# Layer 0 of a four-layer graph network on one core: pair 3 normalised ahead of pair 2 and turned through DRAM, the adjacency's squares turned and written later

## The chip, the cores and the metric

The kernel runs on one core of a Trainium2 chip. The number that counts is device microseconds of one execution, as a median over several; four runs of the kernel before gave 964.04, 964.34, 964.43 and 965.01 us, median 964.38 us. The engines are named as in the profile: PE (matrix products and their weight loads, PEld), DVE (VectorE), ACT (ScalarE), POOL (GpSimd), SP (the engine that issues all the DMAs here).

## What is computed

`x` is 32 graphs of 512 nodes with 128 features, `adj` one 512x512 matrix that all graphs share. Four layers follow each other, each of the form `x = x + layer(relu(layernorm(x)), adj)`. Only layer 0 is touched:

```
h = jnp.maximum(_layernorm(x, axis=-1), 0.0)
# layer 0, with h as input
h0 = jnp.einsum('bnf,fg->bng', input, W[0])
h1 = jnp.einsum('bnf,fg->bng', input, W[1])
m = adj > 0
idx = jnp.cumsum(m.reshape(-1).astype(jnp.int32)) - 1
vals = e[0][idx].reshape(adj.shape)
A = jnp.where(m, vals, jnp.float32(NEG))
A = jax.nn.softmax(A, axis=1)
M = jnp.eye(adj.shape[0], dtype=A.dtype)
out = jnp.einsum('ij,bjg->big', A * M, h0) + jnp.einsum('ij,bjg->big', A * (1.0 - M), h1)
return out + bias[None, None, :]
```

Layer 1 is a Chebyshev filter on `adj`, layer 2 message passing with `adj` squared element by element, layer 3 attention whose weights are multiplied by `adj` (there the transposed `adj` is needed, which layer 0 prepares).

## The kernel before, in words

Two graphs make a pair, so there are 16 pairs, 0 to 15. A quad tile of `x` holds two pairs; layer 0 handles one such tile in each of eight rounds (`round0(r)`, pairs A = 2r and C = 2r + 1).

What one pair needs in layer 0, in this order:

- its statistics (`stats_steps`): four `bn_stats` on DVE (L227), a square root on ACT (L233), then a reciprocal (L235) and the shift `sh` (L236) on DVE;
- the normalised tile `h` (`normed_steps`, L247): eight activations on ACT, four for each graph;
- the same with features on the partitions, `hT`. This is made in one of two ways. `pe_steps` (L261) does eight 128x128 transposes on PE into two PSUM banks (L265) and two copies out of them (L268). `turn_steps` (L278) turns 32x32 squares on DVE, two instructions (L283), writes them with four DMAs into a bounce buffer in DRAM (L290) and reads the whole back with one DMA (L292);
- its projection `g = h W[1]` (`project_steps`): sixteen products on PE (L435) into two banks, two copies on ACT (L460);
- with the round's other pair, four block differences of `g` on POOL (`right_steps`, L356), and `hd`, `hT` scaled by the diagonal of A (`straight`, L703), also on POOL.

A round multiplies the off-diagonal attention by `g` with seven block products instead of eight (Winograd's form); the left sums are made once, the right differences per round. A product with number k goes into bank a, c or d (`ORDER`, L359), and `evict` (L782) takes it out on DVE. Bank c is used three times in a round: product 7 is added on top of product 6 only after DVE has read product 6 out (L787), and product 4 on top of product 7 only after L791. The order on PE in round 0 is 1, 2, 6, 5, 7, 4, 3, and 1, 6, 5, 7, 2, 4, 3 in the others. Between the products come the projections of the next round's pairs and the products with the diagonal (L759).

The order of the instructions in layer 0 is written out by hand: `manual_schedule` (L166) keeps PE, DVE, ACT and POOL in program order, and the loop over `products` in `round0` says at each index i what is issued after the product. The DMAs around the change are kept in program order on SP's queue too. Each engine runs its own list in order, so an instruction that waits holds up all that stands behind it on that engine.

In the kernel before, pairs 0 to 3 are turned on PE and pairs 4 to 15 through DRAM. Pair 2's statistics run ahead of pair 3's (`early_stats_2`, then `ln3`). `turn_adj` (L479) turns `adj` in 32x32 squares: four DVE instructions (L484) and four DMAs to DRAM (L488), all within the preparation and round 0. From round 3 on POOL changes `adj_s` in place for layer 1 (`late_sums`), and the tile `adj_squares` shares its memory with the last tile of `x`, which is loaded at the end of round 3.

Of the kernel before, what the change touches and what calls it, by code (L numbers as in the profile page):

```python
# [24 lines left out]
def kernel(  # L25
# [37 lines left out]
    nc = tc.nc  # L63
    B, N, D = x.shape
    NT = N // P
# [192 lines left out]
    def feature_major(name):  # L258
        return work.tile([P, NQR, 2, P], F32, tag="hT", name=name, bufs=4)
# [53 lines left out]
    def att_copies(*which):  # L313

        for j, half, copy in which:
            copy(attT[:, j, half * H : half * H + H], pt[j][:, half * H : half * H + H])
# [150 lines left out]
    def go(steps, n=99):  # L467
        for _ in range(n):
            if next(steps, steps) is steps:
                return  # L470
# [8 lines left out]
    def turn_adj():  # L479


        ab = last.tile([P, N // QR, NT, QR], F32, tag="x", name="adj_squares")
        for t in range(NT):
            nc.vector.transpose(ab[:, :, t, :], adj_s[:, t, :].rearrange("p (j c) -> p j c", c=QR))  # L484
            yield
        for b in range(NQR):
            tc.keep_in_program_order(
                nc.sync.dma_start(adjT_d[:, blk(b)].rearrange("(j r) e -> r j e", r=QR),  # L488
                                  ab[b * QR : (b + 1) * QR].rearrange("r j t c -> r j (t c)")))
        yield  # L490

# [62 lines left out]
            nc.gpsimd.tensor_sub(ecoln, ecoln, part)  # L556
        parts.append(part)
    h = {q: normed_tile(q) for q in range(3)}
    hT = {q: feature_major(f"hT0_{q}") for q in range(4)}
    normal = [normed_steps(q, h[q]) for q in range(3)]  # L560
    go(normal[0])

# [81 lines left out]
    def scaled_rows(t):  # L644
# [5 lines left out]

    attT = square_tile("attT")
    squares = turn_adj()
    early_stats_2 = stats_steps(2)
    score_rows(0)
    softmax_rows(0)
    next(project[0])
# [13 lines left out]
    softmax_rows(3)  # L670
    inverse(2)
    scaled_rows(2)
    go(early_stats_2, 2)
    inverse(3)
    scaled_rows(3)
    next(project[1])
# [5 lines left out]
    next(left_of_att)  # L682
    att_copies((0, 0, nc.scalar.copy), (1, 0, nc.vector.tensor_copy),
               (2, 0, nc.scalar.copy), (3, 0, nc.scalar.copy))
    go(early_stats_2, 3)
    next(squares)
    go(right_of(0))

    prep_scope.close()
# [30 lines left out]
        tc.keep_in_program_order(nc.gpsimd.tensor_scalar(th[:, 2, :], th[:, 2, :], 2.0, None, OP.mult))  # L720

    ahead = {q: stats_steps(q) for q in range(4, NQ)}
    ln3 = stats_steps(3)
    own, turning, hd, adiag = {}, {}, {}, []
    sums_ahead = late_sums()

    def normalise(q):
        h[q] = normed_tile(q)
        go(normed_steps(q, h[q]))
# [6 lines left out]
        return turning[q]  # L736

    def projection(q):
        return project_steps(q, hT[f"hT0_{q}"] if q > 3 else hT[q])

    def diagonal_of(r, b):
        for q in (2 * r, 2 * r + 1):
            src = hT[f"hT0_{q}"] if q > 3 else hT[q]
            hd[q, b] = straight(src, b, adiag[0], f"hd_{q}_{b}")

    def x_block(r, I, b):
# [15 lines left out]
    def round0(r):  # L762
# [41 lines left out]
        def upper(p):  # L804
            diagonal(p, 0, 0, False)
            nc.vector.tensor_add(x_of(0, 0), of_pairs(halves(p)), x_of(0, 0))

        def add(I, b, i):
            nc.gpsimd.tensor_add(x_of(I, b), x_of(I, b), of_pairs(u[i]))
# [5 lines left out]
        for i, _ in enumerate(products(f"l0_{r}", by_token, sums["att"], now, evict,  # L815
                                          ORDER if r else ORDER0)):
            if r == 0:
                if i == 0:
                    transpose_rows(pt, att, 2)
                    transpose_rows(pt, att, 3)  # L820
                    att_copies((0, 1, nc.scalar.copy), (1, 1, nc.vector.tensor_copy))
                    next(left_of_att)
                    next(left_of_att)
                    go(early_stats_2)
                    att_copies((2, 1, nc.scalar.copy), (3, 1, nc.scalar.copy))
                elif i == 1:
                    for t in range(NT):
                        nc.tensor.matmul(p_adiag[:, blk(t)], ones, diag[:, t, :], start=True, stop=True)
                    nc.scalar.copy(adiag[0], p_adiag)  # L829
                    go(normal[2], NT + 1)  # L830
                    diagonal_of(0, 0)
                    go(ln3, NT + 1)
                    go(normal[2])
                    next(left_of_att)
                    next(left_of_att)
                    next(squares)
                    go(ln3)
                elif i == 2:
                    diagonal_of(0, 1)
                    add(1, 0, 0)  # L840
                elif i == 3:
                    next(turned[2])
                    go(turned[2])
                    add(0, 1, 1)
                    bias(0)
                    normalise(3)
                    go(ahead[4], NT)
                    go(squares)
                elif i == 4:
                    upper(held["a"])  # L850
                    turned.append(pe_steps(h[3], "hT0_3", hT[3]))
                    next(turned[3])
                    go(ahead[4])
                    add(1, 1, 2)
                    go(turned[3])
                    go(projection(2))
                    normalise(4)
                    go(ahead[5], NT)
                    bias(1)
                    go(turn(4))  # L860
                    go(ahead[5])
                elif i == 5:
                    go(projection(3))
                    go(right_of(1))
                    diagonal_of(1, 0)
                    normalise(5)
                elif i == 6:
                    go(stats_c, NT)
                continue
            if i == 0:  # L870
                if C + 2 < NQ:
                    go(turn(C + 2))
                if A + 4 < NQ:
                    normalise(A + 4)
                diagonal_of(r, 1)
                add(1, 0, 0)
            elif i == 1:
                add(0, 1, 1)
                go(stats_a, NT + 1)
                go(own_a, NT)  # L880
                if more:
                    bias(r + 1)
                go(stats_a)
                go(own_a)
            elif i == 2:
                if more:
                    go(projection(A + 2))
            elif i == 3:
                add(1, 1, 2)
                if not more:  # L890
                    next(next_layer)
                if C + 4 < NQ:
                    normalise(C + 4)
                if r >= 3:
                    go(sums_ahead, 2)
            elif i == 4:
                if A + 4 < NQ:
                    go(turn(A + 4))
            elif i == 5:
                if more:  # L900
                    go(projection(C + 2))
                    go(right_of(r + 1))
                    diagonal_of(r + 1, 0)
                go(stats_c, NT + 1)
                go(own_c, NT)
            elif i == 6:
                go(stats_c)
        p = bank(f"p_l0_{r}_e")
        diagonal(p, 1, 1, True)
        nc.vector.tensor_add(x_of(1, 1), of_pairs(halves(p)), x_of(1, 1))  # L910
# [285 lines left out]
```

## Time and profile before

| | before |
|---|---|
| median of four runs | 964.38 us |
| profiled execution, its own time | 964.04 us |
| its span | 962.2 us |
| PE busy | 953.4 us (99%) |
| PEld (weight loads, beside PE) | 781.0 us (81%) |
| DVE / ACT / POOL busy | 585.3 / 469.6 / 421.6 us |
| granted TensorE clock, mean | 0.999 |
| one execution of layer 0: rounds 0 to 7 | from about 29 to 184 us of the span |

Times in the timeline are microseconds from the start of the span: start, duration, engine, line, operation, and what is written and read. Instructions that follow each other with the same line and shape are merged (x8), and an engine's next start can lie a little before the end of the last one, since they are pipelined. A square bracket at the end tells how long the engine sat idle before it and what ended that. SPq lines are the issuing of a DMA, not its data.

### The profile page before, as it was taken

How to read it: one execution, taken by the hardware profiler on the slowest of the kernel's cores; microseconds unless marked ns; L12 is line 12 of the kernel's file. 1: busy time of each engine (PE TensorE's matmuls, PEld its weight loads, DVE VectorE, ACT ScalarE, POOL GpSimd, SP SyncE). 2: the span in 40 equal slices, each digit the busy share in tenths (PEclk: the TensorE clock that was granted, in tenths of full speed). 3: DMA queues.
4: the chain of work that ended last, by engine and by line, in shares of the span. 5: the costliest groups of instructions: out<-in, count | busy, mean ns of one | idle time of the engine just before them, and what ended most of it. 6: DMA issues, size and time to landing. Idle time of an engine off the chain costs nothing.

```text
span 962.2 us, 15160 instructions
## 1 busy us (share of the span) xinstructions
PE 953.4 (99%) x5468; PEld 781.0 (81%) x5469; DVE 585.3 (61%) x1332; ACT 469.6 (49%) x1055; POOL 421.6 (44%) x463
## 2 busy tenths in 40 slices
PE   8999999999999999999999999999999999999998
PEld 4899999898989999899878777777677777767776
DVE  8878885846536546657667665665654444444444
ACT  5865442442232233277627655444765445544553
POOL 4878987833517522513333444433032223223322
PEclk9999999999999999999999999999999999999999
DMA  9257533341341230443333432223121121211111
GB/s 254 59 158 193 154 111 87 98 113 54 105 137 43 68 88 23 110 110 94 87 101 99 126 89 86 70 85 88 55 89 56 56 77 44 76 57 45 55 33 44
DMA packets 83913, 86.04 MB, mean 89 GB/s; under 512 B 6784, under 2 KB 74624, under 8 KB 83840
## 3 DMA queue, kind: packets, MB, share of 16 engines
q1 hardware_dynamic: 83840, 85.09, 31.6%
q8 instruction: 43, 0.70, 0.3%
q14 instruction: 30, 0.25, 0.1%
HBM read 44.17 MB, written 40.89 MB: 88 GB/s over the span
## 4 chain that ended last, share of the span: by engine, by line
PE 96%; ACT 1%; DMA 1%; DVE 1%; issue 0%; SPq 0%; DVEq 0%; ACTq 0%
PE p_av L1116 12%; PE p_score L1101 11%; PE p_l_c L386 8%; PE p_w L435 6%; PE p_l_d L386 6%; PE p_msgT_c L379 5%; PE p_l_a L386 4%; PE p_x1T_c L379 4%; PE p_l L435 3%; PE p_feat L435 3%; PE p_hv L435 3%; PE p_msgT_d L379 3%; PE p_msgT_a L379 3%; PE p_phi L1071 3%; PE p_qkh L1088 3%; PE p_phi L1072 3%
## 5 line engine op out<-in xcount | busy, mean ns | idle before, releaser
L247 ACT ACTIVATE h<-x,sh,rs 128x128 f32<-128x128 f32 x512 | 209.1, 485 | 50.9 <-PE p_x1T_d L379 21.6
L1106 POOL TENSOR_TENSOR ex<-ex,adjTx 128x512 f32<-128x512 f32 x62 | 80.4, 1297 | 208.2 <-ACT ex L1104 208.2
L1102 ACT ACTIVATE ex<-p_score 128x512 f32<-128x512 f32 x128 | 71.9, 587 | 122.8 <-issue 113.0
L1116 PEld LDWEIGHTS p_av<-qkh_hv,ex 128*128 128x128 f32 x1024 | 118.4, 191 | 8.4 <-issue 7.4
L1116 PE MATMUL p_av<-qkh_hv,ex 128*128 128x129 f32 x1024 | 119.9, 274 | 0.0
L1101 PE MATMUL p_score<-qkh_hv,hT 128*128 128x512 f32 x256 | 115.2, 593 | 0.0
L283 DVE STREAM_TRANSPOSE hb_hT<-h 128x512 f32<-128x512 f32 x120 | 82.0, 698 | 23.6 <-ACT h L247 23.3
L1106 DVE TENSOR_TENSOR ex<-ex,adjTx 128x512 f32<-128x512 f32 x66 | 46.2, 703 | 81.7 <-ACT ex L1104 81.7
L227 DVE BATCH_NORM_STATS2 bn<-x 128x6 f32<-128x256 f32 x248 | 89.7, 418 | 0.6
L1101 PEld LDWEIGHTS p_score<-qkh_hv,hT 128*128 128x128 f32 x256 | 46.2, 190 | 46.5 <-issue 44.7
L1104 ACT ACTIVATE ex<-ex 128x512 f32<-128x512 f32 x128 | 76.7, 630 | 1.9
L356 POOL TENSOR_TENSOR rt_feat<-feat,feat 128x256 f32<-128x256 f32 x16 | 11.6, 728 | 136.0 <-ACT feat L1055 136.0
L949 ACT COPY w<-p_w 128x512 f32<-128x512 f32 x32 | 18.2, 574 | 106.1 <-PE p_w L435 106.1
L356 POOL TENSOR_TENSOR rt_w<-w,rt_w 128x512 f32<-128x512 f32 x16 | 20.3, 1272 | 110.3 <-DVE rt_w L356 92.0
L435 PE MATMUL p_w<-th,x1T 128*128 128x128 f32 x256 | 49.5, 275 | 0.0
L435 PE MATMUL p_w<-th,hs 128*128 128x128 f32 x256 | 49.5, 275 | 0.0
L435 PEld LDWEIGHTS p_hv<-vw,hT 128*128 128x128 f32 x256 | 33.6, 192 | 15.3 <-issue 8.1
L1066 POOL TENSOR_TENSOR x<-x,phi2b 128x256 f32<-128x256 f32 x64 | 44.5, 728 | 0.0
L435 PEld LDWEIGHTS p_w<-th,hs 128*128 128x128 f32 x256 | 39.9, 192 | 0.7
L1055 ACT ACTIVATE feat<-feat 128x512 f32<-128x512 f32 x32 | 20.1, 630 | 41.4 <-DVE feat L1054 41.4
L1121 DVE SCALAR_TENSOR_TENSOR x<-p_av,rsum,x 128x128 f32<-128x128 f32 x128 | 39.1, 347 | 1.9
L703 POOL TENSOR_TENSOR hd<-hT,adiag 128x512 f32<-128x512 f32 x32 | 39.7, 1276 | 0.3 <-ACT adiag L829 0.3
(234 smaller groups left out, 2038.6 us busy)
## 6 DMA issues: line engine op xcount, KB each, us to landing
d_hT<-hb_hT SPq DMA_DIRECT2D x240, 128.0 KB
hT<-d_hT SPq DMA_DIRECT2D x60, 512.0 KB
x<-in_x_dram SPq DMA_DIRECT2D x32, 256.0 KB
out_dram<-x SPq DMA_DIRECT2D x31, 256.0 KB
adj_s<-in_adj_dram SPq DMA_DIRECT2D x4, 256.0 KB
adjT_d<-adj_squares SPq DMA_DIRECT2D x4, 256.0 KB
sq<-in_adj_dram SPq DMA_DIRECT2D x4, 256.0 KB
adjTx<-adjT_d SPq DMA_DIRECT2D x4, 256.0 KB
```

The lines of the kernel that those rows point to most:

```text
L227: nc.vector.bn_stats(st[:, k].rearrange("p e s -> p (e s)"), xt[q][:, b, t : t + 2, :].rearrange("p t f -> p f t"))
L247: nc.scalar.activation(h[:, b, t, :], xt[q][:, b, t, :], AF.Relu, bias=shift[q][:, i : i + 1], scale=scale[q][:, i : i + 1])
L283: nc.vector.transpose(hb[:, :, b].rearrange("p j t r -> p t j r"), h[:, b].rearrange("p t (j c) -> p t j c", c=QR))
L379: nc.tensor.matmul(p[:, :H], b[:, k, :], a[:, k, :], start=(first and k == 0), stop=(k == 1), skip_group_check=True)
L386: nc.tensor.matmul(p[:, i * 2 * D : (i + 1) * 2 * D], a[:, k, blk(i)], b[:, k], start=(first and i == 0 and k == 0), stop=(k == 1), skip_g ...
L435: nc.tensor.matmul(p[:, blk(t)], hT(t), w, start=(i == 0), stop=(i == len(terms) - 1))
L1066: tc.keep_in_program_order(nc.gpsimd.tensor_add(xi, xi, spread(phi2b, 2)))
L1101: nc.tensor.matmul(ps, hT[:, t, b, :], qkh, start=True, stop=True)
L1102: nc.scalar.activation(ex[:, t, :], ps, AF.Tanh, scale=1.0 / (8.0 * math.sqrt(D)))
L1104: nc.scalar.activation(ex[:, t, :], ex[:, t, :], AF.Exp, scale=8.0)
L1106: eng.tensor_mul(split(ex[:, t, :]), split(ex[:, t, :]), crossed(adjTx[0][:, t, :]))
L1116: nc.tensor.matmul(po[:, i, : D + 1], ex[:, t, blk(i0 + i)], hv[:, t, :], start=(t == 0), stop=(t == NT - 1))
```

## The change

Pair 3's statistics are begun first and pair 2's follow. Pair 3 is normalised after the first product of round 0, before pair 2, and turned by `turn_steps`: two DVE instructions, four DMA writes and one DMA read in place of eight PE transposes and two ACT copies. Pair 2 stays on PE, and its eight transposes move from before product 7 to behind it. The two ACT copies of the last attention columns move from before pair 2's normalisation at index 0 to index 1. Pair 4's statistics are finished before product 4. The two projections of round 1's pairs now stand together after product 4.

The four square transposes of `adj` leave the preparation and round 0; `turn_adj` now yields after each DMA as well, and rounds 1 and 2 take two steps at each of two places: in round 1 two transposes after index 3 (behind the eviction of product 7) and two after index 6 (behind product 3), in round 2 two DMA writes at each of the same places.

```diff
@@ turn_adj
             tc.keep_in_program_order(
                 nc.sync.dma_start(adjT_d[:, blk(b)].rearrange("(j r) e -> r j e", r=QR),
                                   ab[b * QR : (b + 1) * QR].rearrange("r j t c -> r j (t c)")))
-        yield
+            yield
@@
-    hT = {q: feature_major(f"hT0_{q}") for q in range(4)}
+    hT = {q: feature_major(f"hT0_{q}") for q in range(3)}
@@ preparation
-    early_stats_2 = stats_steps(2)
+    ln2, ln3 = stats_steps(2), stats_steps(3)
...
-    go(early_stats_2, 2)
+    go(ln3, 2)
...
-    go(early_stats_2, 3)
-    next(squares)
+    go(ln3, 3)
+    go(ln2, NT)
     go(right_of(0))
...
-    ln3 = stats_steps(3)
@@ round0, r == 0
                     att_copies((0, 1, nc.scalar.copy), (1, 1, nc.vector.tensor_copy))
+                    next(ln2)
+                    go(ln3)
                     next(left_of_att)
                     next(left_of_att)
-                    go(early_stats_2)
-                    att_copies((2, 1, nc.scalar.copy), (3, 1, nc.scalar.copy))
+                    h[3] = normed_tile(3)
+                    normal.append(normed_steps(3, h[3]))
+                    go(normal[3], NT)
                 elif i == 1:
...
                     nc.scalar.copy(adiag[0], p_adiag)
-                    go(normal[2], NT + 1)
+                    go(normal[3])
+                    go(ln2)
                     diagonal_of(0, 0)
-                    go(ln3, NT + 1)
-                    go(normal[2])
                     next(left_of_att)
                     next(left_of_att)
-                    next(squares)
-                    go(ln3)
+                    go(turn(3))
+                    att_copies((2, 1, nc.scalar.copy), (3, 1, nc.scalar.copy))
                 elif i == 2:
+                    go(normal[2])
                     diagonal_of(0, 1)
                     add(1, 0, 0)
+                    go(ahead[4], NT)
                 elif i == 3:
-                    next(turned[2])
-                    go(turned[2])
                     add(0, 1, 1)
                     bias(0)
-                    normalise(3)
-                    go(ahead[4], NT)
-                    go(squares)
+                    go(ahead[4])
                 elif i == 4:
+                    next(turned[2])
                     upper(held["a"])
-                    turned.append(pe_steps(h[3], "hT0_3", hT[3]))
-                    next(turned[3])
-                    go(ahead[4])
+                    go(turned[2])
                     add(1, 1, 2)
-                    go(turned[3])
-                    go(projection(2))
                     normalise(4)
                     go(ahead[5], NT)
                     bias(1)
                     go(turn(4))
                     go(ahead[5])
                 elif i == 5:
+                    go(projection(2))
                     go(projection(3))
                     go(right_of(1))
@@ round0, other rounds
             elif i == 3:
                 add(1, 1, 2)
+                if r in (1, 2):
+                    go(squares, 2)
...
             elif i == 6:
                 go(stats_c)
+                if r in (1, 2):
+                    go(squares, 2)
```

Where `hT[q]` was chosen for q up to 3 and `hT["hT0_q"]` above, the border is now 2. The products of layers 1 to 3 are not touched.

More of the change, by code (lines that the diff above doesn't have):

```diff
@@ L738, in projection @@
     def projection(q):
-        return project_steps(q, hT[f"hT0_{q}"] if q > 3 else hT[q])
+        return project_steps(q, hT[f"hT0_{q}"] if q > 2 else hT[q])
     def diagonal_of(r, b):
         for q in (2 * r, 2 * r + 1):
-            src = hT[f"hT0_{q}"] if q > 3 else hT[q]
+            src = hT[f"hT0_{q}"] if q > 2 else hT[q]
             hd[q, b] = straight(src, b, adiag[0], f"hd_{q}_{b}")
```

## The prediction

> **What bounds the kernel now.** I read the page first (shares of the engines, chain), then the chain of waits in order of time for layer 0, then each engine's timeline for rounds 0 to 2, and last the DMA share in half-microsecond windows.
>
> ```profile
> PE 953.4 (99%) x5468; PEld 781.0 (81%) x5469; DVE 585.3 (61%) x1332; ACT 469.6 (49%) x1055; POOL 421.6 (44%) x463
> PE 96%; ACT 1%; DMA 1%; DVE 1%; issue 0%; SPq 0%; DVEq 0%; ACTq 0%
> ```
>
> PE is busy 99% and is 96% of the chain that ends last. So a change is worth what it takes from or adds to PE's list, plus the waits it makes or ends there. From 29 us to the end of layer 0 that list runs without a gap but for one stretch, seen in PE's timeline:
>
> ```profile
> 38.31 1.04 PE L265 MATMUL p_hT<-ident,h 128*128 128x128 f32 x8
> 39.19 1.89 PE L386 MATMUL p_l_c<-rt_g,attT 128*128 128x256 f32 x8
> 40.92 1.05 PE L759 MATMUL p_l_a<-w,hd 128*128 128x128 f32 x8
> 41.81 1.68 PE L265 MATMUL p_hT<-ident,h 128*128 128x128 f32 x8
> 43.32 1.95 PE L435 MATMUL p_g<-w,hT 128*128 128x128 f32 x16
> ```
>
> Pair 2's eight transposes take 39.19 - 38.31 = 0.88 us of PE's list; pair 3's take 43.32 - 41.81 = 1.51 us, as they wait for ACT, which normalises pair 3 from 39.91 us for 3.19 us. So 1.51 us is all that can be won here: 0.88 of work, 0.63 of wait.
>
> DVE sets the price on the other side. Its timeline and POOL's at product 7 of round 2:
>
> ```profile
> 79.68 0.18 DVE L235 RECIPROCAL rs<-sd 128x8 f32<-128x8 f32 x1
> 79.90 0.96 DVE L236 SCALAR_TENSOR_TENSOR sh<-bn,rs 128x8 f32<-128x8 f32 x1
> 80.79 0.19 DVE L235 RECIPROCAL rs<-sd 128x8 f32<-128x8 f32 x1
> 81.01 1.08 DVE L236 SCALAR_TENSOR_TENSOR sh<-bn,rs 128x8 f32<-128x8 f32 x1
> 82.02 0.68 DVE L791 TENSOR_TENSOR u_l<-p_l_c,u_l 128x512 f32<-128x512 f32 x1
> ...
> 79.55 2.52 POOL L809 TENSOR_TENSOR x<-x,u_l 128x512 f32<-128x512 f32 x2
> 82.01 1.30 POOL L445 TENSOR_TENSOR x<-x,b 128x512 f32<-128x512 f32 x1
> ...
> 83.57 1.89 PE L386 MATMUL p_l_c<-rt_g,attT 128*128 128x256 f32 x8
> ```
>
> The reader is to see three things. L236 on 128x8 takes 0.17 us where POOL is idle (at 49.84 us) but 0.96 and 1.08 here, and its end falls on the end of a POOL instruction (80.8, 82.05): while a POOL operation runs, this one waits for its end. L791 must be done before PE's product 4 at 83.57; it ends at 82.70, so 0.8 us of slack is left. And DVE has no gap from 71.64 to 83.4 us to absorb a delay.
>
> **Step 1, the transposes go.** PE's list loses eight L265 and the wait: -1.51 us. Two ACT copies of 0.58 us (L268) go too; ACT is off the path, no price of its own.
>
> **Step 2, product 7 comes forward.** With pair 2's transposes behind it, product 7 could start at 38.31. It adds to bank c, so it waits for DVE's L787. In DVE's new list L787 stands behind the two square transposes of pair 3, and the second of these waits for ACT. ACT: `sh` of pair 3 ends about 33.0 (DVE's L785 and copy end at 32.4, L235 and L236 after it until POOL's operation ends at 32.97); four activations at 0.39 us; the diagonal's copy at 35.06 as before, since it waits for PE; four more until 37.2. Second transpose 37.25 to 37.9, L787 37.9 to 38.55, PE at 38.62: a new wait of 0.31 us.
>
> **Step 3, product 4 comes forward.** It waits for L791, which in the new list stands behind pair 4's L235 and L236. Those wait for ACT's square root, which is behind pair 2's eight activations: these start after two copies at 37.8, end 41.0; square root to 41.2; L235 to 41.4; L236 to 41.9, where a POOL operation ends; L791 to 42.5; PE at 42.6. PE gets there at 38.62 + 1.73 (product 7) + 0.88 (pair 2's transposes, whose last waits for 41.0) + 0.89 (diagonal) = 42.12: a new wait of 0.48 us.
>
> Then product 4, diagonal, two projections, product 3 and two diagonals: 1.73 + 0.89 + 3.57 + 1.73 + 0.89 + 0.89 = 9.70, so round 1 starts at 52.3 against 53.03. Sum of steps 1 to 3: -1.51 + 0.31 + 0.48 = **-0.7 us**. Bounds: -1.51 if both waits stay away, 0 if they are twice as long.
>
> **Step 4, pair 3 through DRAM.** Added: two DVE squares of 0.65 us, four DMA writes, one read. SP's timeline shows such a trip for pair 4, and pair 5's read with the product that needs it:
>
> ```profile
> 49.87 1.75 SPq L290 DMA_DIRECT2D d_hT<-hb_hT  x4
> 53.74 0.34 SPq L292 DMA_DIRECT2D hT<-d_hT  x1
> ...
> 63.29 0.34 SPq L292 DMA_DIRECT2D hT<-d_hT  x1
> ...
> 66.96 1.95 PE L435 MATMUL p_g<-w,hT 128*128 128x128 f32 x16
> ```
>
> From the first write's issue to the read's issue 3.9 us; pair 5's read has moved its data by 66.1 us, 2.8 us after its issue, and DMA ends were seen by SP some 0.7 us later (53.05 to 53.74). With the squares done at 37.9: read issued at 41.9, landed at 45.4. The new list needs it at 47.0: hidden, with 1.6 us to spare. Its cover is product 4 and pair 2's projection. The DMA engines are idle from 30 to 42 us, and the writes of `adj`'s squares that filled them from 42.3 to 48 are gone. SP has nothing before it; pairs 4 and 5 follow some 2 and 1 us earlier than before. Price 0; bounds 0 and 1 us.
>
> **Step 5, the squares of `adj` on DVE.** Out of round 0 they cost nothing and save nothing: L785 waited for PE there anyway (0.63 us of idle behind the first). In round 1 two of 0.65 us each stand behind L792: L806 is 0.8 us late, the next squares too, and L799, which waits for PE at 67.23 (0.72 idle), absorbs it. Queued there: pair 6's squares, and with them its trip and the `x` loads behind it on SP, needed 3 us later. Price 0. The other two stand before L910 at 73.4, in the stretch without a gap. All behind them moves by 1.2: L785, pair 7's squares, L787 (77.0 to 78.4, product 7 starts at 79.23: no wait), the statistics. Then L236 misses the POOL operation that ends at 80.8 and waits for the next end, 82.05, its second for 83.3; L791 83.25 to 83.95, PE at 84.0 instead of 83.57: **+0.45 us**, once. Behind that, L799 waits for PE and DVE is level again. Bounds: 0 (the slack holds) and 1.3 (all of the added work).
>
> [...]
>
> **Step 6, the squares' writes.** In the trace the four take from 42.3 to about 47.9 us at a DMA share of 0.91: 1.4 us each, 2.8 for two. In round 2 the first two are issued behind pair 7's read and the others before the loads of the next quad tile of `x` (L119), 1.7 us of SP's time each pair. Who waits: pair 8's writes (needed 4.5 us later) and, behind the `x` loads, pair 9's. Before, pair 9's read is issued at 101.03, landed by about 104.4, and needed at 105.59: 1.2 us of slack. The loads end about 2.8 later than now and pair 9's writes wait 1 to 2.5 us behind them: a stall between 0 and 1.5 us. Pair 7's read (issued 82.09, landed about 85.5, needed 86.19) comes 1.2 later, while PE is 0.45 later: 0 to 0.5. Pair 5 in the trace had its writes behind `x` loads too and was in time, so I take 0 for both and keep the upper ends.
>
> [...] The trace has 186 GB/s in that stretch, so the measured 2.8 stands.
>
> Past round 3 both programs list the same instructions in the same order on every engine, and PE's list is without gaps, so the shift stays: -0.7 + 0.45 = **-0.25 us**. The profiled execution took 964.04 us (span 962.2 and 1.84 around it), the lowest of the four runs and 0.34 below the median. 964.04 - 0.25 = 963.8; against the median, **964.1 us**.
>
> **Rivals.** (A) The waits of steps 2, 3 and 5 are covered: DVE and ACT come earlier than I have them. For it: each wait is only 0.3 to 0.5 us long. Against: DVE, ACT and POOL all have to be early for it. -0.7 to -1.5, 962.9 to 963.7. (B) The waits of round 0 eat the gain, since pair 2 is now normalised last and its last activation (41.0) meets its transposes with nothing to spare: 0 to +0.5, 964.4 to 964.9. (C) The other side: the squares' writes in round 2 delay the trips of pairs 7 and 9 past PE's need. It decides against the change once the stalls exceed 0.25 us, and beyond 0.2% at 2.2. At the top, 1.5 for pair 9 and 2.8 for pair 7 (its read shared with two writes) make 964.1 + 4.3 = 968.4; at the middle, 966. For it: pair 7 has only 0.7 us of slack. Against: pair 7's read is issued before the writes, and pair 5 survived the like. (D) Pair 3's trip lands late and takes the place of the wait removed: it would need 1.6 us; +0.5 beyond that gives 964.6. Against: idle DMA engines.
>
> **How the numbers follow.** 0.2% is 1.9 us, about what a measurement of this kernel can tell from no change. Forecast 0.50, A 0.15, B 0.10, C 0.20, D 0.05. All of the forecast, A, B and D lie within 0.2%; C is split, 0.10 within and 0.10 slower. More than 1.51 us can't be won by these steps: faster 0.02, taken from A; slower 0.11 with a hundredth of D; same 0.87. The range goes from the whole 1.51 us won (962.9) to the middle of C (966.1).
>
> **What would show it.** In the new profile: L265 with eight instructions fewer; PE's product 7 of round 0 near 38.6 and product 4 near 42.6, each after a short idle ended by DVE; round 1 near 52.3; pair 3's L292 near 41.9 and no wait of PE on it; in round 2 an idle of 0.4 us before product 4, ended by DVE L791; no other PE wait in layer 0. Wrong if PE waits for an L292, if the DVE delay goes on past round 2, or if round 1 starts later than 53.

## The result and the profile after

The changed kernel takes 966.14 us (median of 41 runs), the kernel before 964.83 us (median of 61 runs beside them). The ratio is 1.0013, 95% interval [1.0008, 1.0017]: 0.8 to 1.6 us slower. Forecast were 964.1 us and a range up to 966.1, so the time lies just outside the range and the sign of the change is wrong. The profiled execution took 965.98 us with a span of 964.2.

First the engines' busy time and the chain that ends last, from the page of the changed kernel:

```profile
PE 954.6 (99%) x5460; PEld 780.3 (81%) x5461; DVE 587.6 (61%) x1334; ACT 468.8 (49%) x1053; POOL 421.6 (44%) x463
PE 91%; POOL 3%; DVE 2%; issue 1%; DMA 1%; ACT 1%; SPq 0%; POOLq 0%; DVEq 0%; ACTq 0%
```

PE has lost the eight transposes, and its share of the chain has gone from 96% to 91%: the chain now leaves PE in places. The waits of PE from the first product to the end of layer 1's first pairs say where (columns: who waited for whom, total us, times, longest):

```profile
PE p_l_c L386 <- DVE u_l L790: 0.5, 2, 0.3
PE p_l_c L386 <- DVE u_l L786: 0.3, 1, 0.3
PE p_g L435 <- DMA hT<-d_hT: 0.3, 1, 0.3
PE p_x1T_c L379 <- DVE x1T L402: 0.2, 1, 0.2
```

In the kernel before the same view has only the last row, with the same 0.2. (Lines of the changed kernel are one below those of before in this part: L786 is L787 of before, L790 is L791.) The first three rows are in rounds 0 and 2. PE's list has no second path, so the difference can be read off as the length of each round, from the start of its first product to that of the next; "layer 1" is the stretch from its first `p_x1T` to its first product with weights. A second profile of each kernel stands beside the first:

| us | first product | round 0 | round 1 | round 2 | rounds 3 to 6 | layer 1 |
|---|---|---|---|---|---|---|
| before | 29.36 | 23.67 | 19.23 | 19.23 | 19.23 each | 25.74 |
| before, again | 30.03 | 23.66 | 19.24 | 19.23 | 19.23 each | 25.75 |
| after | 29.91 | 23.46 | 19.23 | 20.25 | 19.24 each | 26.06 |
| after, again | 29.80 | 23.04 | 19.24 | 20.09 | 19.23 each | 26.09 |

Round 0 gains 0.2 or 0.6, round 2 loses 1.0 or 0.9, layer 1 loses 0.33. One stretch more differs, behind the table: from the end of PE's last product to the end of the span it is 3.40 us in both profiles of before and 3.71 and 3.72 in those of after. With it the parts add up to +1.4 and +0.9 us, and the spans counted from the first product differ by 1.4 and 0.8. The start differs by chance: it ran from 29.32 to 30.39 us over sixteen profiles, by 0.67 between two of the very same kernel before, so the 0.55 us between the first two profiles is not the change.

**Round 0.** PE's timeline of the changed kernel, with start, busy time and, in brackets, the idle time before it:

```profile
39.61 1.97 PE L386 MATMUL p_l_c<-rt_g,attT 128*128 128x256 f32 x8 [0.34 <-DVE u_l L786]
41.41 1.04 PE L265 MATMUL p_hT<-ident,h 128*128 128x128 f32 x8
...
43.56 1.99 PE L386 MATMUL p_l_c<-rt_g,attT 128*128 128x256 f32 x8 [0.22 <-DVE u_l L790]
45.39 1.05 PE L758 MATMUL p_l_c<-w,hd 128*128 128x128 f32 x8
46.28 3.74 PE L435 MATMUL p_g<-w,hT 128*128 128x128 f32 x32
```

Both forecast waits are there, each ended by the instruction that the forecast named. Why they come late in this profile shows in DVE's timeline, one row of POOL's between:

```profile
33.17 1.27 DVE L236 SCALAR_TENSOR_TENSOR sh<-bn,rs 128x8 f32<-128x8 f32 x1
34.36 0.74 DVE L331 TENSOR_TENSOR sums_att<-p_attT,attT 128x256 f32<-128x256 f32 x2
...
33.15 1.27 POOL L356 TENSOR_TENSOR rt_g<-g 128x512 f32<-128x512 f32 x1
...
38.17 0.71 DVE L283 STREAM_TRANSPOSE hb_hT<-h 128x512 f32<-128x512 f32 x1 [0.15 <-ACT h L247]
38.81 0.65 DVE L786 TENSOR_TENSOR u_l<-p_l_c,u_l 128x512 f32<-128x512 f32 x1
```

L236 of pair 3 started 0.02 us after a POOL operation and lasted as long as that, 1.27 us. In the second profile of the same program it met the end of one:

```profile
33.06 0.32 DVE L236 SCALAR_TENSOR_TENSOR sh<-bn,rs 128x8 f32<-128x8 f32 x1
...
32.09 1.27 POOL L356 TENSOR_TENSOR rt_g<-g,rt_g 128x512 f32<-128x512 f32 x1
```

Round 0 is 0.42 us shorter in that profile, and product 7 starts 9.30 us behind the first product instead of 9.70. Both rows agree with the forecast's reading, that L236 waits for the end of a running POOL operation: L236 ended 0.02 us behind POOL's operation in each (34.44 against 34.42, and 33.38 against 33.36).

**Pair 3's trip** through DRAM, on SP's queue:

```profile
39.04 1.79 SPq L290 DMA_DIRECT2D d_hT<-hb_hT  x4
44.32 0.34 SPq L292 DMA_DIRECT2D hT<-d_hT  x1
```

The read is issued 5.3 us after the first write, not 3.9. The projections of pairs 2 and 3 (46.28, 32 products) run without a gap here and in the second profile (45.76): the trip is hidden, but only just, as run 3 below shows.

**Round 2**, PE, DVE and SP of the changed kernel:

```profile
84.33 1.99 PE L386 MATMUL p_l_c<-rt_g,attT 128*128 128x256 f32 x8 [0.25 <-DVE u_l L790]
86.16 1.05 PE L758 MATMUL p_l_c<-w,hd 128*128 128x128 f32 x8
87.48 2.02 PE L435 MATMUL p_g<-w,hT 128*128 128x128 f32 x16 [0.27 <-DMA hT<-d_hT]
...
73.75 1.29 DVE L484 STREAM_TRANSPOSE adj_squares<-adj_s 128x512 f32<-128x512 f32 x2
...
82.59 1.08 DVE L236 SCALAR_TENSOR_TENSOR sh<-bn,rs 128x8 f32<-128x8 f32 x1
83.60 0.68 DVE L790 TENSOR_TENSOR u_l<-p_l_c,u_l 128x512 f32<-128x512 f32 x1
...
83.46 0.34 SPq L292 DMA_DIRECT2D hT<-d_hT  x1
83.86 0.95 SPq L488 DMA_DIRECT2D adjT_d<-adj_squares  x2
```

The next group starts 1.73 us after a product where there is no gap, and 0.89 after a group of eight diagonal products. So PE loses 0.42 us before product 4 (84.33 against 83.02 + 0.89) and 0.43 before pair 7's projection (87.48 against 86.16 + 0.89). The group behind each wait takes about 0.1 us longer than without one (86.16 - 84.33 = 1.83 instead of 1.73), which makes up the 1.0 us. The second wait is on pair 7's read, behind which two writes of the squares are issued 0.4 us later.

### The profile page after: what moved, and what is told of

Read it like the earlier page. It is cut to its first block, busy times and chain, and to the rows that moved or that the text cites. A ratio compares the mean times of both kernels' runs of the same rounds, so it can differ in the third digit from the quotient of the medians.

```text
span 964.2 us, 15151 instructions
## 1 busy us (share of the span) xinstructions
PE 954.6 (99%) x5460; PEld 780.3 (81%) x5461; DVE 587.6 (61%) x1334; ACT 468.8 (49%) x1053; POOL 421.6 (44%) x463
## 4 chain that ended last, share of the span: by engine, by line
PE 91%; POOL 3%; DVE 2%; issue 1%; DMA 1%; ACT 1%; SPq 0%; POOLq 0%; DVEq 0%; ACTq 0%
PE p_av L1117 12%; PE p_score L1102 11%; PE p_l_c L386 7%; PE p_w L435 6%; PE p_l_d L386 5%; PE p_msgT_c L379 5%; PE p_x1T_c L379 4%; PE p_l_a L386 3%; PE p_l L435 3%; PE p_feat L435 3%; PE p_hv L435 3%; PE p_msgT_d L379 3%; PE p_msgT_a L379 3%; PE p_phi L1072 3%; PE p_qkh L1089 3%; PE p_phi L1073 3%
```

## The experiments

Theory 1: the squares of `adj` in round 2 cost the time, by DVE and by pair 7's trip. Theory 2: round 0's gain is eaten by DVE. Rivals: the loss is in the start or in round 0; the writes, not the squares, are what counts. Five rounds give an interval of about plus or minus 0.9 us on one median, so differences of 0.3 to 0.5 us are read from the round lengths of the traces, and the medians only have to agree with them. Times are given as the difference to the kernel before in the same set of runs.

**1. The squares alone.** The kernel before, with this and without the `squares` calls of round 0:

```
             elif i == 3:
                 add(1, 1, 2)
+                if r in (1, 2):
+                    go(squares, 2)
...
             elif i == 6:
                 go(stats_c)
+                if r in (1, 2):
+                    go(squares, 2)
```

> The kernel before, with adj's squares alone taken out of round 0 and put where the change has them; pairs 2 and 3 stay as they were. Theory 1 (the second couple of squares, which DVE has to do in round 2 where it has no gap, costs the time: it delays L790 and, with pair 7's squares, pair 7's trip): round 2 takes 20.1 to 20.3 us instead of 19.2, all other rounds as before, and the time is 0.85 to 1.05 us above before. Rival (the loss sits in what the change does to pairs 2 and 3 and to the start): within 0.2 us of before.

Measured: 965.86 us, +1.19, ratio 1.0011 [1.0002, 1.002]. Round 0 23.67, round 2 20.41, all others 19.23, layer 1 25.73. PE waits 0.25 for L790 and 0.43 for pair 7's read. So moving the squares alone loses 1.18 us, all in round 2: theory 1 has the place right, though this run does not separate the squares from their writes. Taking the squares out of round 0 wins nothing there.

**2. The second couple of squares elsewhere,** and each couple of writes one place later:

```
                 add(1, 1, 2)
-                if r in (1, 2):
+                if r in (1, 2, 3):
                     go(squares, 2)
...
                 go(stats_c)
-                if r in (1, 2):
+                if r == 2:
                     go(squares, 2)
```

> The changed kernel, with the second couple of squares put behind the third sum of round 2, as the first couple is in round 1, and each pair of writes one place later. Theory 1: PE's waits in round 2 (0.25 before product 4, 0.27 before pair 7's projection) are gone, round 2 takes 19.2 us, and the time falls about 1.0 us below the changed kernel, to between 0.3 us below and 0.3 us above the kernel before. Rival (the loss is in round 0, or is the longer start-up of 0.55 us): it stays within 0.3 us of the changed kernel.

Measured: 965.51 us, +0.84, ratio 1.0009 [1.0, 1.0018]. Round 2 is back at 19.23, as expected, but round 3 is 19.90. PE and SP of this kernel:

```profile
105.76 2.02 PE L435 MATMUL p_g<-w,hT 128*128 128x128 f32 x16 [0.43 <-DMA hT<-d_hT]
...
90.32 0.97 SPq L488 DMA_DIRECT2D adjT_d<-adj_squares  x2
91.34 3.83 SPq L119 DMA_DIRECT2D x<-in_x_dram  x4
95.52 1.83 SPq L290 DMA_DIRECT2D d_hT<-hb_hT  x4
101.71 0.34 SPq L292 DMA_DIRECT2D hT<-d_hT  x1
```

Two writes ahead of the loads of `x` hold pair 9's trip up: 6.2 us from first write to read, where it was 5.25 before (95.78 to 101.03). The loss moved; it did not go. The expected time was missed by that 0.67 and by layer 1's 0.33 (26.07 here).

**3. The squares as in the change, their writes in round 3.**

```
                 add(1, 1, 2)
-                if r in (1, 2):
+                if r in (1, 3):
                     go(squares, 2)
...
                 go(stats_c)
-                if r in (1, 2):
+                if r in (1, 3):
                     go(squares, 2)
```

> The changed kernel with its four transposes of adj where it has them, and all four writes of the squares moved from round 2 to round 3. Theory 1 (pair 7's projection waits since DVE makes its squares 1.2 us later): both waits of PE in round 2 stay, and the time is the changed kernel's within 0.15 us. Rival (forecast's rival C: the writes share the DMA queues with pair 7's trip): the wait before product 4 stays, that before pair 7's projection goes, and the time is 0.3 to 0.45 us below the changed kernel.

Measured: 966.77 us, +2.10, ratio 1.0024 [1.0015, 1.0033]. PE and SP of this kernel:

```profile
84.21 1.99 PE L386 MATMUL p_l_c<-rt_g,attT 128*128 128x256 f32 x8 [0.23 <-DVE u_l L790]
86.04 1.05 PE L758 MATMUL p_l_c<-w,hd 128*128 128x128 f32 x8
86.93 1.95 PE L435 MATMUL p_g<-w,hT 128*128 128x128 f32 x16
...
83.33 0.34 SPq L292 DMA_DIRECT2D hT<-d_hT  x1
86.72 1.75 SPq L290 DMA_DIRECT2D d_hT<-hb_hT  x4
...
SPq L119 <- DMA adjT_d<-adj_squares: 3.9, 1, 3.9
114.68 2.04 SPq L119 DMA_DIRECT2D x<-in_x_dram  x4
...
127.15 2.02 PE L435 MATMUL p_g<-w,hT 128*128 128x128 f32 x16 [1.59 <-DMA hT<-d_hT]
```

Pair 7's read is issued as late as in the changed kernel (83.33 against 83.46), but with no writes behind it PE does not wait for it: theory 1 falls on this point, and the rival holds. Round 2 is 19.73, so the squares on DVE cost 0.50 and the writes the rest, 0.52 or 0.36 in the two profiles of the change. Then round 4 takes 21.06 instead of 19.23: pair 11's trip is late, and PE pays 1.8 us for it there. This is not only a matter of shared transfers: the `x` loads ahead of that trip need the memory of `adj_squares`, and SP held them 3.9 us until the writes out of it had landed (the row with L119 <- DMA; in the changed kernel these loads are issued at 110.45). Round 0 of this run, whose instructions there are those of the changed kernel, is 23.40: product 4 is on time (13.24 us behind the first product), but pair 3's read is not, and the 32 projections take 4.09 us instead of 3.74.

**4. Statistics moved in round 0.**

```
-                    att_copies((0, 1, nc.scalar.copy), (1, 1, nc.vector.tensor_copy))
-                    next(ln2)
                     go(ln3)
+                    att_copies((0, 1, nc.scalar.copy), (1, 1, nc.vector.tensor_copy))
+                    next(ln2)
...
                     bias(0)
-                    go(ahead[4])
                 elif i == 4:
+                    go(ahead[4])
```

> The changed kernel with two steps of statistics moved on DVE in round 0: pair 3's L235 and L236 ahead of the copy of attT, so that L236 starts inside another POOL operation than the one that blocked it for 1.27 us, and pair 4's L235 and L236 behind L790 and L791. Theory 2 (round 0's gain of 1.51 us is eaten by DVE: L236 held by POOL, then L786 late, then L790 behind pair 4's statistics): PE's waits of 0.34 and 0.22 us, with the refill of the array behind each, are gone, and the time is 0.6 to 1.0 us below the changed kernel. Rival (the start-up takes it): the waits go and the time stays within 0.2 us, or new waits on ACT's activations or pair 3's read take their place: 0 to 0.3 us below.

Measured: 965.09 us, +0.42, ratio 1.0004 [0.9995, 1.0012]; the changed kernel is at +1.2 to +1.3 in its own sets. Round 0 is 22.80, 0.24 to 0.66 below the changed kernel's. The wait before product 4 is gone; that before product 7 is 0.20, since pair 3's two squares still stand ahead of L786 and DVE has no gap up to there; and the trip of pair 3 now shows, 0.2 us inside the projections. Round 2 keeps its loss (20.23). What the expectation calls a refill of the array is, in the changed kernel's round 0, a group that takes 1.80 and 1.83 us behind the two waits (39.61 to 41.41, 43.56 to 45.39) instead of 1.73; no run shows why. Theory 2 holds for the cause, with a smaller size: the medians differ by 0.8 to 0.9, but 0.33 of this is layer 1's delay, which this program does not have (experiment 8).

**5. Both mended:** the statistics of run 4, squares at the third sum of rounds 1 and 2, one write at the end of round 2 and three behind the third sum of round 3.

```
                 add(1, 1, 2)
                 if r in (1, 2):
                     go(squares, 2)
+                elif r == 3:
+                    go(squares)
...
                 go(stats_c)
-                if r in (1, 2):
-                    go(squares, 2)
+                if r == 2:
+                    next(squares)
```

> The changed kernel with both moves of statistics of the round-0 run, the second couple of squares behind the third sum of round 2, and the writes spread: one at the end of round 2, three behind the third sum of round 3. Theory (round 0's DVE order, the squares in round 2 and their writes ahead of a pair's trip are all of the loss, beside 0.33 us in layer 1 that no step explains): round 0 takes 22.8 us, rounds 1 to 7 as before, no wait of PE on a read; the time is 0.5 to 0.9 us below the kernel before (964.67). Rival (each write costs its 0.6 us per couple wherever a trip follows it): a wait on the read of pair 9 or 11 of 0.2 to 1.6 us is left, and the time is within 0.3 us of before or above.

Measured: 963.98 us, -0.54, ratio 0.9995 [0.9986, 1.0004]. Round 0 is 22.78, every other round as before, no wait on a read past round 0. The single write ahead of the `x` loads fits into pair 9's slack, the three behind pair 9's read into pair 10's.

> The kernel of the fifth run unaltered, for a narrower interval and a second look at round 0: rounds 22.7 to 23.1 us in round 0, 19.23 from 1 to 6, and 0.4 to 0.9 us below the kernel before.

Measured: 964.07 us, -0.78, ratio 0.9992 [0.9983, 1.0001]; round 0 22.72. Both intervals still touch 1.

**6. Pairs 2 and 3 alone,** the squares and writes back in round 0:

```
     go(ln2, NT)
+    next(squares)
...
                     go(turn(3))
+                    next(squares)
...
                     bias(0)
+                    go(squares)
                     go(ahead[4])
```

> The changed kernel with adj's squares and their writes back in round 0 (one square ahead of the right-hand sums, one behind pair 3's squares, two ahead of pair 4's reciprocal, then the four writes): pairs 2 and 3 alone are changed. Theory (the loss is the squares' move): round 2 takes 19.2 us, round 0 between 23.4 and 23.9 as the squares fill DVE's wait for ACT there, and the time is within 0.3 us of the kernel before. Rival (adj's writes had to leave round 0, since they share the DMA queues with pair 3's read): PE waits 0.5 to 1.2 us for pair 3's read before its projection, round 0 takes 24.2 to 25, and the time is 0.5 to 1.3 us above before.

Measured: 965.56 us, +1.04, ratio 1.0011 [1.0002, 1.0021]. Round 0 is 24.35, round 2 19.23. PE of this kernel:

```profile
32.77 1.99 PE L386 MATMUL p_l_a<-g,attT 128*128 128x256 f32 x8 [0.48 <-DVE u_l L785]
...
39.89 1.97 PE L386 MATMUL p_l_c<-rt_g,attT 128*128 128x256 f32 x8 [0.78 <-DVE u_l L787]
...
48.37 2.05 PE L435 MATMUL p_g<-w,hT 128*128 128x128 f32 x16 [0.33 <-DMA hT<-d_hT]
```

Both answers are in part right: two waits on DVE, which has no room for the squares beside pair 3's, and one on pair 3's read, behind which the four writes are issued 0.45 us later. So once pair 3 is turned by DVE, the squares cannot stay at these places of round 0; others there were not tried with the trip.

**7. Pair 3 early, but turned by TensorE** (`turned.append(pe_steps(h[3], "hT0_3", hT[3]))` and `go(turned[3])` behind pair 2's in place of `go(turn(3))`):

> The changed kernel with pair 3 turned by TensorE again, its early normalisation kept: eight L265 more on PE behind pair 2's, and DVE without pair 3's two squares. Theory (the trip is hidden and is worth the 0.88 us of PE, but pair 3's squares hold L786 up): PE's wait of 0.34 us before product 7 goes, 0.88 us of transposes come, round 0 takes 23.7 to 23.95 us, and the time is 0.2 to 0.5 us above the changed kernel. Rival (the trip costs nothing and saves nothing, since PE waits there anyway): round 0 as in the changed kernel, 23.4 to 23.5.

Measured: 964.67 us, +0.15, ratio 1.0002 [0.9993, 1.0011]. Round 0 is 23.13 (round 2 keeps its loss, 20.34): with eight transposes more on PE it is 0.33 below the changed kernel's first profile and 0.09 above its second. That is below both answers, nearer to the rival's. In run 11, where nothing else disturbs, PE's timeline shows why:

```profile
38.74 1.89 PE L386 MATMUL p_l_c<-rt_g,attT 128*128 128x256 f32 x8
40.47 1.15 PE L265 MATMUL p_hT<-ident,h 128*128 128x128 f32 x8
41.45 1.06 PE L758 MATMUL p_l_a<-w,hd 128*128 128x128 f32 x8
42.34 1.04 PE L265 MATMUL p_hT<-ident,h 128*128 128x128 f32 x8
43.22 1.89 PE L386 MATMUL p_l_c<-rt_g,attT 128*128 128x256 f32 x8
```

Without pair 3's squares on DVE, L786 is in time for product 7 (38.74, no wait). Pair 3's transposes (42.34) fill the time in which product 4 would wait for L790. The trip takes 0.88 us from PE and gives nearly all of it back as these two waits.

**8. The 0.33 us of layer 1.** The instructions of that stretch are the same in both kernels and no step of the forecast reaches it. DVE's L402 of layer 1's second pair in the changed kernel:

```profile
197.86 0.42 DVE L402 TENSOR_TENSOR x1T<-p_x1T_c,x1T 128x256 f32<-128x256 f32 x1 [1.71 <-PE p_x1T_c L379]
```

Its idle time is 1.71, in the kernel before 1.35, with PE and ACT at the same distance. Over the programs it goes by the place of this instruction in DVE's compiled list, event waits counted: delayed at place 439 (the changed kernel, runs 2, 3 and 6), not at 434 (runs 7, 9, 11), 435 (before, run 1) or 440 (runs 4 and 5). Run 8 is the changed kernel with one memset of 128x1 more on DVE in round 5:

```
+                if r == 5:
+                    nc.vector.memset(stats.tile([P, 1], F32, tag="extra", name="extra", bufs=1), 0.0)
```

> The changed kernel with one more instruction on DVE, a memset of 128x1 at the start of round 5, where DVE has gaps. In the programs run so far the 0.33 us in front of layer 1's second pair is there when that L402 is instruction 439 of DVE's main list (the changed kernel twice, the runs of spread squares, later writes and pair 3 alone) and not when it is instruction 434, 435 or 440. Theory 3 (DVE's place in its code): with 440 the stretch takes 25.73 us instead of 26.06, and the time is 0.2 to 0.4 us below the changed kernel. Rival (it comes from the order of the work in front): it stays at 26.06.

Measured: 966.02 us, +1.17, ratio 1.0009 [1.0, 1.0017]. The same row of this kernel, and a row 338 us later, of layer 2:

```profile
196.90 0.42 DVE L402 TENSOR_TENSOR x1T<-p_x1T_c,x1T 128x256 f32<-128x256 f32 x1 [1.36 <-PE p_x1T_c L379]
...
534.73 0.42 DVE L402 TENSOR_TENSOR msgT<-p_msgT_c,msgT 128x256 f32<-128x256 f32 x1 [0.66 <-ACT msgT L400]
```

Layer 1's stretch is 25.71: the delay is gone, by one harmless instruction. But now the second row is late, 0.66 of idle where the changed kernel's second profile has 0.48, and PE loses 0.2 there; runs 4 and 5 have that too. This L402 is at place 951 of DVE's list: 439 + 512. The expected 0.2 to 0.4 us on the median was not seen, as 0.2 of it comes back and the interval is wider than the rest.

**9. The order alone:** run 7 with the squares in round 0, two ahead of pair 4's reciprocal and two behind L791, then the writes.

> Pair 3 normalised ahead of pair 2 as in the changed kernel, but turned by TensorE, and adj's four squares in round 0 where DVE waits for ACT (two) and behind L790 and L791 (two), their writes behind them. Theory (the order alone is worth what the change can win, the trip through DRAM and the squares' place add nothing): round 0 takes 23.1 to 23.4 us, rounds 1 to 7 as before, layer 1's stretch 25.73; the time is 0.3 to 0.6 us below before. Rival (the squares in round 0 delay DVE or pair 4's trip): a wait of PE at product 3 or at pair 4's read in round 1, time at before or above.

Measured: 964.19 us, -0.66, ratio 0.9992 [0.9984, 1.0001]. Round 0 is 23.13, so the squares are free there, but round 1 is 19.75: PE waits 0.28 us for pair 5's read, as the four writes (issued from 44.91) set pair 4's trip, the `x` loads and pair 5's trip back. The second answer has the right mechanism, one pair further on.

**10. Run 5 with two memsets more on DVE,** as in run 8, which puts the two L402 at places 441 and 952:

> The kernel of round0_and_spread with two memsets of 128x1 added on DVE in round 5, which put L402 of layer 1's second pair at place 441 of DVE's list and that of p_msgT at 952. Theory 3 (the delay of 0.35 us sits at places 439 and 951 of DVE's code, whatever stands there, and costs PE only where that instruction is an L402 itself): neither stretch has a delay, the stretch of layer 1 takes 25.73 us and p_msgT_c is not late; rounds as in round0_and_spread; 0.6 to 1.0 us below the kernel before. Rival (the two delays are properties of these two places of the program): one of them is back, 0.3 us more.

Measured: 963.71 us, -1.06, ratio 0.9988 [0.9979, 0.9997]. Layer 1's stretch is 25.74 and the row of layer 2 is in time:

```profile
532.89 0.43 DVE L402 TENSOR_TENSOR msgT<-p_msgT_c,msgT 128x256 f32<-128x256 f32 x1 [0.49 <-ACT msgT L400]
```

Neither delay is left, as the place in the list says. This is the one version of eleven whose interval lies below 1: 0.3 to 2.0 us below the kernel before. The interval overlaps those of runs 5, 9 and 11, so it is not shown to be better than these. PE in its round 0:

```profile
38.65 1.96 PE L386 MATMUL p_l_c<-rt_g,attT 128*128 128x256 f32 x8 [0.18 <-DVE u_l L786]
...
42.22 1.89 PE L386 MATMUL p_l_c<-rt_g,attT 128*128 128x256 f32 x8
43.95 1.05 PE L758 MATMUL p_l_c<-w,hd 128*128 128x128 f32 x8
44.84 3.94 PE L435 MATMUL p_g<-w,hT 128*128 128x128 f32 x32
```

Product 4 has no wait; 0.18 is left before product 7, and 3.94 instead of 3.74 us for the projections is the late end of pair 3's trip.

**11. Run 7 with the squares and writes of run 5.**

> Pair 3 normalised early but turned by TensorE, with the squares and writes placed as in round0_and_spread. Theory (the trip through DRAM wins nothing here: the 0.88 us of transposes that it saves come back as PE's waits on DVE, which does pair 3's squares): round 0 takes 23.1 us, rounds 1 to 7 19.23 to 15.66 as before, no delay in layer 1; 0.5 to 0.8 us below the kernel before, and within 0.4 us of the run with the trip. Rival (the trip is worth its 0.88 us): 0.9 us above the run with the trip.

Measured: 963.94 us, -0.83, ratio 0.9991 [0.9982, 1.0]. Round 0 23.13, all others as before, layer 1 25.76. Against run 10 (22.78) the trip, together with the moved statistics, is worth 0.35 us of round 0, not 0.88; without the moved statistics it is worth 0.1 at best (23.04 to 23.06 in the second profile of the change and in runs 2 and 8) and less than nothing in the others (23.46 in the first profile, 23.40 in run 3). Nor is that 0.35 seen in the whole: from the first product to the end of the span run 10 takes 932.2 us and run 11 932.1 (before: 932.9 and 932.8). What run 10 wins in round 0 it loses behind PE's last product, where it takes 3.64 us and run 11 3.18. In all ten profiles with pair 3's trip this stretch is 3.63 to 3.72, in those of before and run 1 3.40, in runs 7, 9 and 11 3.18 to 3.21; why is open.

**The two kernels again,** for the table above:

> The changed kernel, unaltered, profiled a second time. If the 0.55 us of the start and the 0.33 us at layer 1's second pair are properties of the program, the first product starts at 29.9 us and the stretch from layer 1's start to its first product of weights takes 26.06 us again; if they are chance, they differ from that by more than 0.1 us.

> The kernel before, profiled a second time: if the first product's start (29.36 us in its first profile, 29.3 to 30.4 in all the others) and round 0 (23.67) are fixed by the program, they come out within 0.05 us of these; if the start is chance, it differs by more than 0.1 us and round 0 does not.

Measured: 965.72 us (+1.20, ratio 1.0013 [1.0003, 1.0023]) for the changed kernel, 964.98 (+0.13, 1.0004 [0.9994, 1.0014]) for the kernel before. The start is chance; round 0 is fixed in the kernel before (23.67, 23.66), and swings by 0.4 in the changed one; layer 1's 0.33 belongs to the program.

## Why the prediction was wrong, step by step

**Step 1 (the transposes go)** and **steps 2 and 3 (two new waits)** were right in mechanism, and in size for one of the two profiles. Counted from the first product, the forecast has product 7 at 9.26 us, product 4 at 13.24 and round 1 at 22.94. The second profile has 9.30, 13.23 and 23.04, the first 9.70, 13.65 and 23.46. The difference is L236 in step 2, which the forecast ends when POOL's operation ends, at 32.97: it starts near the border of two POOL operations, 0.25 us ahead of it in the second profile and 0.02 behind it in the first, and so waits for the end of one or for the whole of the next. I took the cheap side as given and left the other out of the bounds. Of the nine profiles with this order (the change, runs 2, 3, 6, 7, 8, 9 and 11) two have the long side, 0.94 and 1.27 us, the others 0.21 to 0.39.

**Step 4 (pair 3's trip hidden)** was right in price for the two profiles of the change, wrong in slack: the read is issued 5.3 us after the first write instead of 3.9, so the 1.6 us to spare are gone. In run 3 PE waits 0.36 for it, in runs 4 and 10, where product 4 is early, 0.2. What else the experiments show of this step: the 0.88 us that it saves is not a gain by itself, as run 7 gave the same round 0 without it.

**Step 5 (the squares on DVE)** was right: the first couple is absorbed (round 1 at 19.23), the second makes L790 late at the named place, 0.42 us and 0.1 for the slower group behind the wait (0.50 in run 3), forecast 0.45.

**Step 6 (the squares' writes)** is the step that failed. I took 0, with 0.5 as the upper end for pair 7 and 1.5 for pair 9, since pair 7's read is issued ahead of the writes and "pair 5 survived the like". The upper end is what came: 0.36 to 0.52 us for pair 7 (round 2's loss less the 0.50 of the squares), shown by run 3. (The forecast's time at which pair 9 is needed, 105.59, should read 105.43, the start of its projection; that leaves 1.0 us of slack by its own estimate instead of 1.2.) Pair 9 had no wait, but only in this arrangement: with PE earlier (run 2) it costs 0.67. Rival C had the right mechanism and, with pair 7, one of its two places, far below the top of its range; it stood at 0.20 against 0.50 for the forecast. That the time lands on the middle of C, 966, is chance: only these 0.36 to 0.52 us of the miss are C's. Its argument against, that the read goes first, was no argument: the read was issued at 83.46 and PE's projection let go at 87.48, so the writes issued 0.4 us later shared most of its flight.

**That the shift stays** failed too, and for more: 0.33 us in layer 1 and 0.31 behind PE's last product, in both profiles. The forecast let the shift stay since past round 3 both programs list the same instructions in the same order. That does not hold: the same instruction at another place of DVE's list was late (experiment 8), and the closing stretch goes with the program, for a reason that no run shows.

The sum: the forecast's -0.25, with 0.05 more in step 5, 0.36 to 0.52 in step 6, 0.33 in layer 1, 0.31 behind the last product and 0.1 to 0.5 in steps 2 and 3, is +0.9 to +1.5; measured are +0.8 to +1.6. The reference level was a part of the miss too: 964.38 from four runs, 964.83 from 61.

Rival A (the waits are covered) is out: all three came. Rival B (they eat round 0's gain) took 0.5 of the forecast's 0.7 us in one profile and 0.1 in the other. Rival D (pair 3's trip late) did not come in the two profiles of the changed kernel, and came with 0.2 to 0.36 us in runs 3, 4 and 10.

## What to carry to other kernels

Work that is taken off the bound engine is worth what the engine does instead: here two waits on DVE stood ready behind the transposes, so 0.88 us saved were 0.1 of round 0 at best, and 0.35 once the statistics in front of these waits were moved too. A bulk write has to be placed by the transfers that fly beside it and queue behind it, with the slack of each next trip counted in the trace: two writes of 256 KB cost 0.4 to 0.7 us at pairs 7 and 9, while one and three at other places cost nothing. Memory that two tiles share counts as well: the 1.8 us at pair 11 came where a load had to wait for the writes out of its memory to land. An edit that changes the number of instructions on an engine can move delays of 0.2 to 0.35 us to places that it does not touch (run 8), so a difference of that size needs the round-by-round table, a second profile and a version with the list shifted before it is put down to the edit.

## What the runs showed of the hardware that was not expected

A DVE instruction at place 439 of this kernel's list came 0.35 us late in every profile in which an L402 stood there (five, of four programs), and that at 951 some 0.2 us late in the four profiles with an L402 there (runs 4, 5 twice, 8); at 434, 435, 440, 441 and 952 an L402 was in time. The distance is 512. In run 10 the instruction at 1463, which is 512 further (L1112, at 863.89 us), came 0.35 us late against run 11, and PE did not wait for it; at 695 and 1207, half way, no profile has such a delay. No run shows what makes the place matter. The page of the changed kernel lists two queues of the kind "instruction" (packets, MB, share of time):

```profile
q8 instruction: 43, 0.70, 0.3%
q14 instruction: 31, 0.25, 0.1%
```

In the changed kernel no transfer of these two queues runs within 2 us of the late instruction at 197.86.

The length of L236, 128x8 elements, was 0.21 to 1.27 us for pair 3 in round 0, behind the same instruction of DVE's list, by where it met POOL's operations.

A trip through DRAM takes 3.7 to 3.9 us from first write to read in most cases, and 5.1 to 6.0 at pairs 5, 7, 9 and 11 of the kernel before, which stand behind loads of `x`. But pair 3 takes 5.3 with nothing ahead of it on SP, and pair 11 of the changed kernel 3.9 behind such loads. The traces show what goes with the long ones. Of the 64 pieces in which pair 3's four writes land, 63 were there by 42.71 us and the last at 44.19; one transfer of 16 KB on the queue q8 "instruction" ran from 41.88 to 42.98 among them. Over the trips of layer 0 in all sixteen profiles, 63 of the 71 with such a transfer among their writes took 4.7 to 6.8 us, and 126 of the 131 without one 3.7 to 4.3. That the transfer holds one piece up is argued from this; no run moves it.
